# P7 of both layers as an inner Strassen product, and the x1 outer sums on GpSimd, in a two-layer graph kernel

## The chip, the cores and the metric

The kernel runs on one core of a Trainium2 chip. The metric is the device time of one execution in microseconds. The kernel before took 1842.32 us as the median of three runs (1842.28 to 1844.9).

Engine names are those of the profile: PE is TensorE (PEld its weight loads), DVE is VectorE, ACT is ScalarE, POOL is GpSimd, SP is SyncE, which here only issues DMAs.

## What is computed

There are 64 graphs of 256 nodes with 512 features each, all in float32. Two layers follow each other, each with a residual connection and a layer norm:

```python
# layer 0; W is (512, 1024)
deg = jnp.sum(adj, axis=-1, keepdims=True)
agg = jnp.einsum('bij,bjf->bif', adj, x) / jnp.maximum(deg, EPS)
cat = jnp.concatenate([x, agg], axis=2)
x = _layernorm(x + relu(jnp.einsum('bnf,of->bno', cat, W)))
# layer 1; X is the new x
q, k = jnp.split(X @ Wqk, 2, axis=-1)
v = X @ Wv
agg = jnp.einsum('bij,bjd->bid', adj, k * mask[:, :, None])
w = inv_scale * mask * jnp.einsum('bid,bid->bi', q, agg)
x = _layernorm(X + softmax(w, axis=1)[:, :, None] * v)
```

## The kernel before

**Algebra.** In layer 0, W splits into a half that acts on x and a half whose product with x is gathered by adj. In layer 1, Wqk is first folded into one 512 x 512 matrix (`weight_product`), so that q times the gathered k becomes x1 times the gathered product. Each layer therefore has one product of x, or x1, with a 512 x 1024 weight, and one product of adj with a result (`gather`). Each of these is done by the Winograd form of Strassen's scheme: seven products P1 to P7 in place of eight, at the cost of sums of the operands and of the results.

**Outer and inner.** The weight product is split into 2 x 2 blocks; this is the outer step. One of its products has a stationary operand from x of 256 features by 256 rows (128 of each of two graphs) and a weight block of 256 x 512. `outer` (line 619) does it directly, as four matmuls of 128x128 by 128x512, two for each graph. `inner` (line 551) does it by a second step of the same scheme, whose rows are the two graphs, whose contraction halves are the two chunks of 128, and whose columns are the two halves of 512: seven matmuls of 128x128 by 128x256. `INNER` (line 26) lists for each layer the products that are inner ones. P6 and P7 are outer in both layers; `product` (line 614) chooses, and takes `outer` as long as the weight's inner sums don't exist (`sides[p]` is not yet a dict).

**What an inner product needs.** Its weight sums are made once, in `weight_sums` (line 466), by VectorE, or by GpSimd for the products in `W1_BY_GP`. Layer 1's sums of the products in `FULL_FIRST` are kept back in `waiting_sums` and made within the second iteration (line 1025), so that the first pair's layer 1 does these as outer products. Its input sums are made for every pair by GpSimd in `inner_sums` (line 512): four additions of 128x128 for each product, or of 128x256 for P1 and P2 together. In `inner`, each matmul writes half of a scratch bank, and ACT and VectorE carry the result to the target banks `q`. For P4, P6 and P7 (`also`) the target already holds a partial sum:

```python
def third():
    mm(lo, s(2), b["T3"])
    if also:
        vec.tensor_add(halves(q[1]), halves(q[1]), twice(kept(lo)))
```

Here `kept` is an ACT copy of 256 columns into a `fifth` buffer. In all, an inner product with `also` has four such copies, four VectorE additions of 256 columns and one of 512. The sums of the outer step are made in `outer_sums` (line 502), three additions of 512 columns: for x by GpSimd, but for the very first pair, and for x1 by VectorE (line 1008, and in the last pair's part). The fourth one is made in `fourth_sums` by GpSimd.

**Order of the work.** The loop runs over 32 pairs of graphs. An iteration interleaves layer 0 of pair j with layer 1 of pair j-1. The order of PE's units is written out by hand in strings: `ORDER0` and `ORDER1` for the first two iterations, `ORDER` for the others, `ORDER9` for the last pair's layer 1. Each letter is one unit of a product:

- layer 0: i, k, m, p, q, r, s are P1, P5, P2, P6, P7, P3, P4, and a to g are its gather;
- layer 1: J, K, H, Q, N, P, L are P1, P2, P6, P7, P5, P4, P3, and A to G are its gather;
- in the last part, S and Z are two steps of the last softmax.

`take` (line 890) calls the units in this order, and `when` adds work of other engines as soon as named units are done: `start_layer1` after L, P7's input sums of layer 1 after K. Nothing is issued at once. Every instruction goes to the `Plan` (line 75), which gives each a cost and a due time and then writes the order of all engines by list scheduling, PE's included, so that a unit that can't start yet may be passed by a later one. `HOME` and `HOME9` name the scratch bank of each product and each gather, one of eight PSUM banks. [...]

Of the kernel before, what the change touches and what calls it, by code (L numbers as in the profile page):

```python
# [16 lines left out]
P = 128  # L17
Q = 32
# [4 lines left out]
S1, S2, S3, S4 = range(4)  # L23


INNER = (("P1", "P2", "P5", "P3", "P4"), ("P1", "P2", "P5", "P3", "P4"))
SLOTS_X = {"P1": 0, "P2": 1, "P5": 2, "P3": 2, "P6": 0, "P7": 1, "P4": 0}
SLOTS_X1 = {"P1": 0, "P2": 1, "P5": 2, "P6": 0, "P7": 1, **({"P3": 2, "P4": 0} if "P7" in INNER[1] else {"P3": 0, "P4": 1})}
W1_BY_GP = ("P5", "P3", "P4")
HOME = "i6 k7 m6 p2 q0 r7 s6 a7 b2 c3 J6 K2 H4 Q7 N7 L7 P6 A6 B4 C5"  # L30
HOME9 = "J6 K7 H2 Q1 N7 L1 P1 A2 B3 C1"
LATE = 4.0
FULL_FIRST = ("P7", "P4")
ORDER0 = ("k k k k k k i i i i i k i i p p q q r p p r r m m q m m r q m r m r s s s r s m a s b s d s e c "
          "g f")
ORDER1 = ("i k i i i i k k k i k k i p k m m p p r m q p r m r m r q r s r q q s s m r s m s s a J s b d J "
          "J e J J J J c H f H K H K g K Q K K K K C N A Q N N D H N N E N Q B Q P G P N L P L F L P L L L "
          "L")
ORDER = ("i i i k i i k k i i k k k k p p p r q p m m m r m q r m s q r q r s m s s r s s m r a J b J J d "
         "J J J s e c J f H K K H K K g K K N Q K H N Q A D N C E N H Q N G N Q P P F P P P N L L L P P B "  # L40
         "L L L L")
ORDER9 = ("J J A D C E J J J J F J K G B H H K K K H Q K H N Q K Q K P Q N P N P N P P N P P S N N L L L L "
          "Z L L L")


class Step:
# [274 lines left out]
def resnorm_kernel(  # L321
# [13 lines left out]
    B, N, F = x.shape  # L335
    A = wqk_t.shape[0] // 2
    NT, NF, NA = N // P, F // P, A // P
    H, HF = NF // 2, F // 2
# [12 lines left out]
    vec = Recorder(plan, "DVE", nc.vector, vec_cost)  # L351
    act = Recorder(plan, "ACT", nc.scalar, act_cost)
    gp = Recorder(plan, "POOL", nc.gpsimd, gp_cost)
# [110 lines left out]
    waiting_sums = {}  # L464

    def weight_sums(w, name, layer, by_gp=()):
        b11, b21, b12, b22 = (w[:, k * H:(k + 1) * H, :] for k in range(4))
        t1, t2, t4 = (mem.tile([P, H, F], F32, name=f"{name}{k}") for k in (1, 2, 4))
        it = [mem.tile([P, len(INNER[layer]), HF], F32, name=f"{name}i{r}") for r in (1, 2, 4)]
        sides = {"P4": t4, "P6": t2, "P7": b12}  # L470
        sub = vec.tensor_sub

        def inner_of(p, b, later=None):
            later = layer == 1 and p in FULL_FIRST if later is None else later
            if p not in INNER[layer]:
                return
            n = INNER[layer].index(p)
            sub = gp.tensor_sub if p in by_gp else vec.tensor_sub
            c11, c12, c21, c22 = (b[:, e, h * HF:(h + 1) * HF] for e in range(2) for h in range(2))
            i1, i2, i4 = (i[:, n] for i in it)  # L480
            if later:
                waiting_sums[p] = lambda: inner_of(p, b, False)
                return
            sides[p] = {"B11": c11, "B21": c21, "B22": c22, "T3": c12, "T1": i1, "T2": i2, "T4": i4}
            sub(i1, c12, c11)
            sub(i2, c22, i1)
            sub(c12, c22, c12)
            sub(i4, c21, i2)
        sub(t1, b12, b11)
        inner_of("P1", b11)  # L490
        sub(t2, b22, t1)
        inner_of("P5", t1)
        sub(b12, b22, b12)
        sub(t4, b21, t2)
        inner_of("P2", b21)
        inner_of("P6", t2)
        inner_of("P7", b12)
        inner_of("P3", b22)
        inner_of("P4", t4)
        return sides  # L500

    def outer_sums(X, eng):
        eng.tensor_add(X.block(S1), X.block(A21), X.block(A22))
        eng.tensor_sub(X.block(S2), X.block(S1), X.block(A11))
        eng.tensor_sub(X.block(S3), X.block(A11), X.block(A21))
# [421 lines left out]
    for j in range(NP):  # L927
        X = Xs.pop(j)
        own = owns[j] = ring("own", [P, 2, NT, F], 3)
        u, y, o = pf, py, pu  # L930
        ys[j] = ring("y", [P, 2, NT, F])
        at = homes(HOME)
        units, made = layer0(j, X, o, u, y, at), Counter()
        sizes = Counter({name: len(parts) for name, parts in units.items()})
        waiting = []

        def when(done, work):
            waiting.append((full(done, sizes), work))

        def start_gather0():  # L940
            units.update(gather("abcdefg", sumsA.pop(j), sums_T(ys[j]), at["a"], at["c"], at["b"],
                                own=own, rdeg=rdegs.pop(j)))

        def end_gather0():
            place = norm0(j)
            mask_adj(j)
            if place:
                when("P.L" if j else "", place)

        def x_sums(*ps):  # L950
            for p in ps:
                if p in INNER[0]:
                    inner_sums(X, p)

        def next_x():
            if j == 0:
                pass
            elif j < NP - 1:
                load_xT(j + 1)
            if j < NP - 1:  # L960
                inner_sums(Xs[j + 1], None)
                outer_sums(Xs[j + 1], gp)
                inner_sums(Xs[j + 1], "P5")

        def next_adj():
            if j < NP - 1:
                load_adj(j + 1)
                sumsA[j + 1] = adj_sums(j + 1, 0)
        if j > 0:
            load_x(j)  # L970
        if 0 < j < NP - 1:
            load_rows(j + 1)
            degrees(j + 1)
        when("k", lambda: (fourth_sums(X), x_sums("P3")))
        when("i", lambda: x_sums("P6"))
        when("m", lambda: x_sums("P7"))
        when("p" if "P6" in INNER[0] else "i", lambda: x_sums("P4"))
        when("pqr", start_gather0)
        when("rs", next_x)
        when("abcdefg", end_gather0)  # L980
        if j == 0:
            when("abcdefg", next_adj)
        else:
            Y = x1Ts.pop(j - 1)
            u2, o2, y2 = o, pf, y
            vs[j - 1], aggs[j - 1] = v_of(j - 1), agg_of(j - 1)
            q_at = ys[j][:, :, 0]
            new, dots = layer1(j - 1, Y, q_at, o2, u2, y2, at)
            sizes.update({name: len(parts) for name, parts in new.items()})
            made["L"] = sizes["L"] - len(ahead)  # L990
            ahead += new.pop("L")
            units.update(new, L=ahead)

            def y_sums(*ps):
                for p in ps:
                    if p in INNER[1] and isinstance(W1[p], dict):
                        inner_sums(Y, p)

            def start_layer1():
                if j == 1:  # L1000
                    for k in range(2):
                        turn_here(Y, owns[0], k, o)
                    mask_adj(0)
                else:
                    softmax(j - 2)
                sumsM[j - 1] = adj_sums(j - 1, 1)
                inner_sums(Y, None)
                outer_sums(Y, vec)
                inner_sums(Y, "P5")

            def start_gather1():
                units.update(gather("ABCDEFG", sumsM.pop(j - 1), T[0], at["A"], at["C"], at["B"],
                                    aggs[j - 1]))
            when("L" if j > 1 else "m", start_layer1)
            when("J", lambda: y_sums("P6"))
            when("K", lambda: y_sums("P7" if "P7" in INNER[1] else "P4"))
            when("H", lambda: (fourth_sums(Y), y_sums("P4" if "P7" in INNER[1] else "P3")))
            if "P7" in INNER[1]:
                when("HN", lambda: y_sums("P3"))
            T = []  # L1020
            when("ikmpqrs" if j == 1 else "", lambda: T.append(sums_T(owns[j - 1], aggs[j - 1])))
            when("gK", start_gather1)
            when("BFK", dots)
            if j == 1:
                when("QP", lambda: [waiting_sums[p]() for p in sorted(waiting_sums)])
            when("ABCDEFG", next_adj)
        take((ORDER0, ORDER1)[j] if j < 2 else ORDER, units, made, waiting)
        if j > 0:
            py, pu = pu, py
# [34 lines left out]
    def divide():  # L1064
# [12 lines left out]
        ("BFK", dots))]  # L1077
    take(ORDER9, units, Counter(), waiting)
    p = small("probs", [P, 2, NT], 2)
# [51 lines left out]
```

## Time and profile before

| what | value |
|---|---|
| median of the runs | 1842.32 us |
| the profiled execution | 1844.13 us |
| its span, first to last instruction | 1842.4 us |
| granted TensorE clock, mean | 0.997 |
| instructions in the span | 26290 |
| DMA traffic | 181.61 MB, mean 99 GB/s |

The profile is a page on one execution. Its parts used below are: the busy time of each engine with its share of the span; the chain of work that ended last, followed back from the last instruction, as shares by engine; the groups of instructions, each with the tile it writes and those it reads, its shape, its count, its busy time and the mean duration of one in ns, and after the bar the idle time just before them with what ended it; and the waits, as "waiter <- releaser: us in total, times, longest". Since nearly every instruction is issued by one helper, all lines show the same few line numbers, and groups are told apart by their tiles: `bank` is PSUM, `xT` and `x1T` the transposed inputs of the two layers, `_s` their outer sums, `_i` their inner sums, `w` the weights, `t` and `t_i` the weights' sums, `fifth` the copies made by `kept`, `sa` the sums of adj.

### The profile page before, as it was taken

What the parts mean: (1) busy time and instruction counts of PE and PEld (TensorE: products, weight loads), DVE (VectorE), ACT (ScalarE), POOL (GpSimd) and SP (SyncE); (2) the same over time, 40 slices, a digit from 0 to 9 for tenths busy, and PEclk for the clock granted to TensorE, in tenths of its full rate; (3) what the DMA queues carried; (4) which work ended last, traced back from release to release, by engine and by line L of the source; (5) the groups of instructions that cost most, each with busy time, mean ns of one, the idle gap of its engine ahead of it and who ended that gap; (6) DMA issues with size and microseconds to landing.
All of it is one profiled execution on the core that took longest, in us unless ns stands there. A gap on an engine that the chain in (4) does not pass through costs nothing.

```text
span 1842.4 us, 26290 instructions
## 1 busy us (share of the span) xinstructions
PE 1829.1 (99%) x7376; PEld 1381.8 (75%) x7376; DVE 1542.9 (84%) x3397; ACT 1243.4 (67%) x3239; POOL 957.5 (52%) x1519
## 2 busy tenths in 40 slices
PE   9999999999999999999999999999999999999997
PEld 5677777777777777777777777777777777777775
DVE  7888888888889888888888798888888888988877
ACT  3656876667776667766677766677666677666766
POOL 6746454465454564544654545645446545456432
PEclk9999999999999999999999999999999999999998
DMA  6134334334334343343343343433333433434302
GB/s 236 51 76 121 94 93 102 89 108 110 97 81 110 90 118 97 93 98 96 101 114 95 82 107 97 111 99 92 97 99 98 106 104 82 106 97 110 98 13 75
DMA packets 380721, 181.61 MB, mean 99 GB/s; under 512 B 263712, under 2 KB 345248, under 8 KB 380576
## 3 DMA queue, kind: packets, MB, share of 16 engines
q1 hardware_dynamic: 380576, 179.94, 36.6%
q8 instruction: 59, 0.97, 0.2%
q14 instruction: 86, 0.70, 0.1%
HBM read 114.35 MB, written 34.08 MB: 81 GB/s over the span
## 4 chain that ended last, share of the span: by engine, by line
PE 98%; DVE 1%; DMA 1%; ACT 0%; SPq 0%; issue 0%; DVEq 0%; ACTq 0%
PE bank L370 97%; DMA shared<-wqk_t 1%; DVE bank L285 0%; DVE own L285 0%; PE bank L376 0%; SPq L386 0%; ACT own L285 0%; DVE w L285 0%; DVE y L285 0%; DVE x1T_s L285 0%; DVE t L285 0%; ACT fifth L285 0%; DVE x L285 0%; ACT junk L285 0%; ACT bank L285 0%
## 5 line engine op out<-in xcount | busy, mean ns | idle before, releaser
L285 ACT COPY y<-bank 128x512 f32<-128x512 f32 x256 | 146.4, 585 | 369.1 <-PE bank L370 361.5
L285 DVE TENSOR_TENSOR bank<-bank,fifth 128x256 f32<-128x256 f32 x571 | 255.7, 454 | 50.3 <-ACT fifth L285 22.9
L285 POOL TENSOR_TENSOR x1T_i<-x1T 128x256 f32<-128x256 f32 (+1 forms) x126 | 74.8, 605 | 409.4 <-PE bank L370 399.9
L285 ACT COPY shared<-bank 128x512 f32<-128x512 f32 x314 | 183.7, 586 | 74.5 <-PE bank L370 70.3
L370 PE MATMUL bank<-w,x1T 128*128 128x512 f32 (+1 forms) x512 | 207.3, 487 | 1.2 <-DVE own L285 0.7
L370 PE MATMUL bank<-w,xT 128*128 128x256 f32 (+1 forms) x496 | 200.1, 486 | 0.0
L285 ACT ACTIVATE own<-own,shift,rstd 128x512 f32<-128x512 f32 x254 | 197.9, 820 | 1.5 <-DVE shift L285 1.5
L285 ACT ACTIVATE junk<-own,less 128x512 bf16<-128x512 f32 x254 | 183.9, 724 | 4.0
L285 ACT COPY fifth<-bank 128x256 f32<-128x256 f32 x380 | 136.2, 375 | 66.1 <-PE bank L370 62.2
L370 PE MATMUL bank<-t_i,x1T_i 128*128 128x256 f32 x636 | 179.7, 380 | 0.0
L285 ACT COPY bank<-bank 128x256 f32<-128x256 f32 (+1 forms) x352 | 150.5, 428 | 43.0 <-PE bank L370 29.3
L285 DVE SCALAR_TENSOR_TENSOR own<-bank,rdeg,own 128x256 f32<-128x256 f32 x384 | 172.7, 477 | 7.8 <-PE bank L370 2.8
L285 DVE TENSOR_TENSOR shared<-bank,shared 128x512 f32<-128x512 f32 (+1 forms) x157 | 137.7, 892 | 46.4 <-PE bank L370 46.3
L370 PE MATMUL bank<-t_i,xT_i 128*128 128x256 f32 x640 | 165.2, 379 | 0.0
L370 PE MATMUL bank<-t,x1T_s 128*128 128x512 f32 (+1 forms) x384 | 163.6, 521 | 0.6 <-DVE x1T_s L285 0.6
L285 DVE TENSOR_TENSOR y<-bank,y 128x512 f32<-128x512 f32 x192 | 132.0, 688 | 37.1 <-PE bank L370 32.8
L370 PE MATMUL bank<-t,xT_s 128*128 128x512 f32 (+1 forms) x384 | 153.8, 521 | 0.0
L370 PEld LDWEIGHTS bank<-t_i,xT_i 128*128 128x128 f32 x640 | 119.8, 190 | 34.4 <-issue 17.0
L285 POOL TENSOR_TENSOR sa<-adj 128x256 f32<-128x256 f32 x128 | 93.7, 732 | 99.0 <-ACT adj L285 94.5
L285 DVE TENSOR_TENSOR shift<-less,rstd 128x2 f32<-128x2 f32 (+1 forms) x128 | 46.4, 380 | 113.6 <-ACT rstd L285 113.5
L285 POOL TENSOR_TENSOR xT_i<-xT 128x128 f32<-128x128 f32 (+1 forms) x126 | 80.2, 637 | 114.3 <-PE bank L370 103.3
L370 PEld LDWEIGHTS bank<-t_i,x1T_i 128*128 128x128 f32 x636 | 120.1, 190 | 19.7 <-issue 2.2
(170 smaller groups left out, 4589.7 us busy)
## 6 DMA issues: line engine op xcount, KB each, us to landing
x<-x SPq DMA_DIRECT2D x64, 512.0 KB, 3.7
xT<-x_t SPq DMA_DIRECT2D x62, 512.0 KB, 3.8
out<-own SPq DMA_DIRECT2D x62, 512.0 KB, 2.8
x1T<-turn SPq DMA_DIRECT2D x480, 64.0 KB, 2.1
adj<-adj_t SPq DMA_DIRECT2D x64, 256.0 KB, 3.0
turn<-adj SPq DMA_DIRECT2D x64, 256.0 KB, 3.7
turn<-dram SPq DMA_DIRECT2D x31, 264.0 KB, 5.1
shared<-wqk_t SPq DMA_DIRECT2D x4, 512.0 KB, 8.4
```

The costliest lines, as they stand in the source:

```text
L285: self.plan.record(self.name, lambda: call(out, *args, **kwargs), outs, ins, busy, done, port)
L370: plan.record("PE", lambda: nc.tensor.matmul(ps, a, b, start=start, stop=True, skip_group_check=True), [ps], [a, b], busy, busy + 0.165, w ...
```

## The change

P7 becomes an inner product in both layers. This adds its weight sums (layer 1's are made in the second iteration, now after Q, P, N and J in place of Q and P) and its input sums on GpSimd. In layer 1 it also puts P3's and P4's input sums into other slots and makes them one hook later. The x1 outer sums go from VectorE to GpSimd, but for the last pair. The strings that order the units and name the scratch banks are new. The new default in `sides` has no effect on what is issued.

```diff
-INNER = (("P1", "P2", "P5", "P3", "P4"), ("P1", "P2", "P5", "P3", "P4"))
+INNER = (("P1", "P2", "P5", "P3", "P4", "P7"), ("P1", "P2", "P5", "P3", "P4", "P7"))
-HOME = "i6 k7 m6 p2 q0 r7 s6 a7 b2 c3 J6 K2 H4 Q7 N7 L7 P6 A6 B4 C5"
-HOME9 = "J6 K7 H2 Q1 N7 L1 P1 A2 B3 C1"
+HOME = "i6 k7 m7 p0 q6 r7 s6 a7 b2 c3 J3 K2 H5 Q5 N7 L6 P7 A6 B4 C5"
+HOME9 = "J7 K6 H4 Q6 N7 L7 P0 A2 B3 C1"
-ORDER0 = ("k k k k k k i i i i i k i i p p q q r p p r r m m q m m r q m r m r s s s r s m a s b s d s e c "
-          "g f")
-ORDER1 = ("i k i i i i k k k i k k i p k m m p p r m q p r m r m r q r s r q q s s m r s m s s a J s b d J "
-          "J e J J J J c H f H K H K g K Q K K K K C N A Q N N D H N N E N Q B Q P G P N L P L F L P L L L "
-          "L")
-ORDER = ("i i i k i i k k i i k k k k p p p r q p m m m r m q r m s q r q r s m s s r s s m r a J b J J d "
-         "J J J s e c J f H K K H K K g K K N Q K H N Q A D N C E N H Q N G N Q P P F P P P N L L L P P B "
-         "L L L L")
-ORDER9 = ("J J A D C E J J J J F J K G B H H K K K H Q K H N Q K Q K P Q N P N P N P P N P P S N N L L L L "
-          "Z L L L")
+ORDER0 = ("i k k i i i i i k i k k m m m k p m k p m p m m r p q r q q q r r r r q q r q s s s s s a b s s "
+          "d e c f g")
+ORDER1 = ("i k k i i k i k i k i i p m m k k m m p m m p p r r m q q r q r q q r q r q r s s s a J s J s s "
+          "J s b J d J J e c J H f H K K H H K g Q K K K K Q N P C A N B Q D N E Q N G N F N N L L P L P L "
+          "P L L")
+ORDER = ("k k k k i i i L i i i i k m k p k m m p m m q r p p m r r m q q q q q q s s r r s r r s a J s J "
+         "J s s b d J e J g J c f J J K H K H K K H K K K H A N Q Q Q N Q N Q Q N D N C E Q F P P P G P B N "
+         "P N L P L P L L L L")
+ORDER9 = ("J J J J J J J C A D K K E B K K H F G K H Q N H N K H K N N N Q Q Q Q Q N Q P N L P P L L P P P "
+          "L P S L Z L L")
...
-        sides = {"P4": t4, "P6": t2, "P7": b12}
+        sides = {"P1": b11, "P2": b21, "P3": b22, "P4": t4, "P5": t1, "P6": t2, "P7": b12}
...
                 inner_sums(Y, None)
-                outer_sums(Y, vec)
-                inner_sums(Y, "P5")
+                outer_sums(Y, gp)
+                y_sums("P5")
...
-                when("QP", lambda: [waiting_sums[p]() for p in sorted(waiting_sums)])
+                when("QPNJ", lambda: [waiting_sums[p]() for p in sorted(waiting_sums)])
```

More of the change, by code (lines that the diff above doesn't have):

```diff
@@ L29 @@
 W1_BY_GP = ("P5", "P3", "P4")
-HOME = "i6 k7 m6 p2 q0 r7 s6 a7 b2 c3 J6 K2 H4 Q7 N7 L7 P6 A6 B4 C5"
-HOME9 = "J6 K7 H2 Q1 N7 L1 P1 A2 B3 C1"
+HOME = "i6 k7 m7 p0 q6 r7 s6 a7 b2 c3 J3 K2 H5 Q5 N7 L6 P7 A6 B4 C5"
+HOME9 = "J7 K6 H4 Q6 N7 L7 P0 A2 B3 C1"
 LATE = 4.0
 FULL_FIRST = ("P7", "P4")
-ORDER0 = ("k k k k k k i i i i i k i i p p q q r p p r r m m q m m r q m r m r s s s r s m a s b s d s e c "
-          "g f")
-ORDER1 = ("i k i i i i k k k i k k i p k m m p p r m q p r m r m r q r s r q q s s m r s m s s a J s b d J "
-          "J e J J J J c H f H K H K g K Q K K K K C N A Q N N D H N N E N Q B Q P G P N L P L F L P L L L "
-          "L")
-ORDER = ("i i i k i i k k i i k k k k p p p r q p m m m r m q r m s q r q r s m s s r s s m r a J b J J d "
-         "J J J s e c J f H K K H K K g K K N Q K H N Q A D N C E N H Q N G N Q P P F P P P N L L L P P B "
-         "L L L L")
-ORDER9 = ("J J A D C E J J J J F J K G B H H K K K H Q K H N Q K Q K P Q N P N P N P P N P P S N N L L L L "
-          "Z L L L")
+ORDER0 = ("i k k i i i i i k i k k m m m k p m k p m p m m r p q r q q q r r r r q q r q s s s s s a b s s "
[4 more added lines that the diff above has]
+ORDER = ("k k k k i i i L i i i i k m k p k m m p m m q r p p m r r m q q q q q q s s r r s r r s a J s J "
+         "J s s b d e J g J c f J J K H K H K K H K K K H A N Q Q Q N Q N Q Q N D N C E Q F P P P G P B N "
+         "P N L P L P L L L L")
+ORDER9 = ("J J J J J J J C A D K K E B K K H F G K H Q N H N K H K N N N Q Q Q Q Q N Q P N L P P L L P P P "
+          "L P S L Z L L")
 class Step:
```

## The prediction, on record before the result

> **What bounds the kernel now.** I read the page's busy line and its chain of waits first, then busy time by stretch, the order of time on PE, and the groups and waits of the engines that PE depends on.
>
> ```profile
> PE 1829.1 (99%) x7376; PEld 1381.8 (75%) x7376; DVE 1542.9 (84%) x3397; ACT 1243.4 (67%) x3239; POOL 957.5 (52%) x1519
> ...
> PE 98%; DVE 1%; DMA 1%; ACT 0%; SPq 0%; issue 0%; DVEq 0%; ACTq 0%
> ```
>
> PE is busy all the time and carries 98% of the chain that ended last. A busy PE need not be a fast PE, so I looked at where it has gaps:
>
> ```profile
> core 0: us, PE busy (x) PEld busy (x) DVE busy (x) ACT busy (x) POOL busy (x), PEclk, DMA share, GB/s
> 0.00:100.00 100.00, 96.20 (x352) 63.87 (x353) 78.69 (x151) 50.61 (x129) 68.92 (x98) 1.00 0.41 138
> 500.00:1000.00 500.00, 500.00 (x2028) 380.83 (x2027) 423.10 (x940) 342.05 (x899) 261.83 (x420) 1.00 0.38 99
> 1777.00:1842.40 65.40, 55.90 (x227) 40.16 (x226) 44.26 (x110) 45.06 (x117) 17.40 (x30) 0.90 0.16 53
> ```
>
> Only the first 100 us and the last 65 have PE gaps. DVE stands at 423 of 500 us in the steady part. And at what pitch PE runs there:
>
> ```profile
> 600.53 1.03 PE L370 MATMUL bank<-shared,sa 128*128 128x256 f32 x4
> 601.40 0.59 PE L370 MATMUL bank<-t_i,x1T 128*128 128x256 f32 x2
> 601.83 0.59 PE L370 MATMUL bank<-t_i,x1T_i 128*128 128x256 f32 x2
> 602.26 1.02 PE L370 MATMUL bank<-w,x1T 128*128 128x512 f32 x2
> 603.12 1.03 PE L370 MATMUL bank<-shared,adj 128*128 128x256 f32 x4
> ```
>
> Each float32 matmul of the code is two records. The starts differ by 0.43 us for a 256-column matmul (601.40 to 601.83) and 0.86 for a 512-column one (602.26 to 603.12). The medians from record to record over the whole trace are 216 and 429 ns. One pair of graphs in the loop has 32 records of 512 columns (P6 and P7 of both layers) and 196 of 256 (five inner products a layer of 7 matmuls, two gathers of 14): 32 x 0.429 + 196 x 0.216 = 56.06 us, and the 1000 us from 500 on, with 4058 records, lose about 3 us against that pitch. The steady part has no slack: less PE work is less time, as long as the others keep up.
>
> ```profile
> L285 DVE TENSOR_TENSOR bank<-bank,fifth 128x256 f32<-128x256 f32 x508 | 212.3, 425 | 50.1 <-ACT fifth L285 22.7 <-PE bank L370 16.6 <-ACT junk L285 1.7
> L285 DVE TENSOR_TENSOR bank<-bank,fifth 128x512 f32<-128x512 f32 x63 | 43.4, 689 | 0.2 <-ACT fifth L285 0.2
> L285 DVE TENSOR_TENSOR x1T_s<-x1T 128x512 f32<-128x512 f32 x32 | 22.2, 693 | 0.1
> L285 POOL TENSOR_TENSOR xT<-xT 128x512 f32<-128x512 f32 x30 | 38.5, 1284 | 0.0
> L285 POOL TENSOR_TENSOR x1T_i<-x1T_s 128x128 f32<-128x128 f32 x128 | 59.6, 467 | 29.2 <-DVE x1T_s L285 26.8
> ```
>
> These are the prices of what the change adds and moves. Last, what DVE waits for from 500 to 1500 us, and one wait of PE's weight load:
>
> ```profile
> DVE shift L285 <- ACT rstd L285: 65.2, 34, 3.6
> DVE shared L285 <- PE bank L370: 27.0, 17, 1.6
> DVE y L285 <- PE bank L370: 18.3, 37, 0.6
> DVE bank L285 <- ACT fifth L285: 11.4, 18, 0.6
> ...
> PEld bank L370 <- POOL xT_i L285: 11.0, 17, 0.7
> ```
>
> [...] of 355 such DVE additions of 512 columns, the 214 that overlap no GpSimd instruction took 682 ns on average, the 141 that do 933. [...]
>
> **The change, part by part.**
>
> *PE.* P7 as an outer product is 8 records of 512 (3.43 us); as an inner one, 14 of 256 (3.02): 0.41 us less. It applies to 32 pairs in layer 0 and to 31 in layer 1, since the first pair's layer 1 is built before the weight sums of P7 exist. 63 x 0.412 = **26.0 us** off PE. A pair goes from 56.06 to 55.24 us.
>
> *DVE.* Inner P7 accumulates on banks that already hold P6, so each of its scratch results is copied by ACT and added by DVE: four additions of 256 and one of 512, 4 x 0.425 + 0.689 = 2.39 us, 4.78 a pair. The x1 outer sums leave: 3 x 0.697 = 2.09. Net +2.69. Contention now costs DVE some 91 us in all (the excess of overlapped over free durations, the 512 ns excess of the tiny shift products included), 2.9 a pair; with GpSimd busier by a quarter and fewer DVE targets I add 0.3. DVE work a pair is 0.848 x 56.06 = 47.5, so 50.5 of 55.24 us: 91%. It lies beside PE's work; that is the cover, and its loss is the first rival below.
>
> *ACT.* Four copies of 375 ns a P7: +3.0 us a pair, 38.4 to 41.4 of 55.2 (75%). They are queued with norm's squares and its rstd, for which DVE's shift waits. I charge nothing: ACT still idles a quarter of the time; uncovered it is up to 3 us a pair.
>
> *GpSimd.* The three outer sums come to 3 x 1.284 = 3.85 us, the sums of P7's inputs to 8 x about 0.5 = 4.0: 29.2 to 37.1 a pair, 67%. What is queued behind the outer sums is P5's sums (4 x 0.467) and later those of P4, P7, P3; in exchange GpSimd's own wait for DVE's S1 (26.8 us in the row above) goes. Covered, since in the new order J comes 39 units of at least 0.43 us, 17 us, after the L that starts them; uncovered, P5 would be 1.8 us later (3.85 against 2.09).
>
> *Scratch banks.* P7 of both layers now needs one (q6, Q5), shared with i6 and s6, and with the gather's C5. A P7's units can't run tighter than matmul, copy, next matmul; the trace has no such inner P7. Bounds: 0 if other products lie between, as they do for P4 now, to about 0.3 us for each of three reuses (copy 0.375 plus the matmul's tail, less one unit of 0.43), 0.9 a product, 1.8 a pair. For this and all other small waits of the steady part I take 0.15 us a pair near the lower end, because units of N, r or p can be put between: 30 x 0.15 = **+4.5 us**.
>
> *Head.* Layer 0's P7 weight sums are four more DVE subtractions of 256 (the t_i and w rows of the first 35 us take 0.41 to 0.67): 2.1 us, plus 2.39 for the first q, in 100 us with 78.7 of DVE work and 3.8 of PE gaps. Between 0 and 4.5; I take **+1.5**. Layer 1's sums come at about 140 us behind other DVE work, first read by the next pair: nothing.
>
> *Tail.* The last pair has 2.39 us more on DVE, where DVE and ACT set the end from 1818 us on (0 to +3). Against this its new order leaves 3 L units after S in place of 9 N and L units, and those 9 ran from 1825 to 1834.5 with gaps: S comes some 2 us later, what follows ends some 4 earlier (-2). I take 0.
>
> *Orders.* Otherwise the same units in new places: no charge beyond the 0.15 above, as the old order left PE without gaps and the new one must be as good; uncovered, that is the rivals. DMA volume and SP's queue don't change.
>
> *Sum.* The profiled execution took 1844.13 us (span 1842.4, 1.7 around it): 1844.1 - 26.0 + 4.5 + 1.5 + 0 = 1824.1. It lies 1.8 above the median of the runs shown, 1842.32, so in terms of the median **1822.3**.
>
> **Rivals.**
>
> *DVE becomes the bound (slower).* DVE idles about 7.5 us a pair at waits, 3.65 of them with shift at the head of its queue until ACT has rstd (65.2 us over 17.8 pairs). DVE work 50.5 + 0.3 of small gaps + waits: if the waits stay over 5.3 us a pair, the pair is longer than 56.06 and the gain is gone. At 6 us: 56.8, +0.75 x 30 = +22, and with the head +1.5, near 1866. For it: shift's wait isn't one for PE, and ACT gets 3 us more ahead of it; DVE is at 94 to 100% in more than half of the stretches of 4 us of a pair. Against it: waits for PE shrink by themselves when DVE is behind, and most norm and transpose work of DVE isn't urgent.
>
> *GpSimd comes late (gain half lost).* PE's weight load already waits 0.65 us once a pair for a sum by GpSimd, just hidden. With 7.9 us more on that queue, 0.4 us more of it uncovered costs 30 x 0.4 = 12: about 1834. For it: GpSimd is at 90 to 100% in some stretches of a pair. Against it: its longest wait, for PE, is 13 us once a pair.
>
> *P7 isn't replaced.* Only so for the first pair's layer 1, counted above.
>
> **Chances and range.** Forecast, 1814 to 1830: 0.50. GpSimd or bank waits, 1830 to 1846: 0.20, of which 0.12 still faster. DVE-bound, slower: 0.30, half of it over 1862. A measurement of this kernel tells about 0.2%, 3.7 us, from no change. So faster 0.62, same 0.08, slower 0.30. The low end takes no stalls and the better tail (1844.1 - 26.0 - 2 - 1.8 = 1814); the high end goes into the slower case to leave out less than 0.2.
>
> **What would show it.** Right: 256-column records up by 882, 512 down by 504; PE without gaps from 100 us to the tail, a pair near 55.3 us; DVE at 91% and GpSimd at 67% there, DVE's waits for PE smaller. Wrong: PE gaps every pair released by DVE bank (first rival) or by POOL x1T_i or xT_i (second), or by ACT fifth (scratch bank), each read as PE idle over 30 pairs; head and tail by the first 100 and last 65 us.

## The result and the profile after

The changed kernel takes 1842.75 us (median of 12 runs, 1842.14 to 1843.51); beside it the kernel before takes 1842.7 us (12 runs, 1841.92 to 1844.9). The ratio is 0.9999, 95% interval 0.999 to 1.0008: no change, where a gain of 20 us was forecast. The profiled execution took 1842.84 us, its span is 1841.0 us.

Busy line and chain shares of the page, after:

```profile
PE 1818.4 (99%) x7754; PEld 1433.2 (78%) x7754; DVE 1672.4 (91%) x3627; ACT 1332.0 (72%) x3491; POOL 1269.4 (69%) x1864
...
PE 96%; DVE 2%; ACT 1%; DMA 0%; issue 0%; POOL 0%; SPq 0%; ACTq 0%; DVEq 0%
```

378 records of 882 - 504 more: the replacement of P7 happened in full. DVE is at 91% and GpSimd at 69%, as forecast. PE is still busy 99% and still carries the chain. Yet 26 us of its work are gone and the time stayed, so PE got slower somewhere. Busy time by stretch (columns as in the prediction) shows only part of where:

```profile
0.00:100.00 100.00, 94.31 (x358) 64.34 (x359) 80.99 (x158) 49.90 (x127) 73.08 (x102) 1.00 0.39 133
500.00:1000.00 500.00, 500.00 (x2147) 397.75 (x2146) 462.22 (x1003) 370.62 (x974) 353.53 (x521) 1.00 0.38 101
1777.00:1841.00 64.00, 49.00 (x225) 39.34 (x223) 46.74 (x115) 45.38 (x121) 18.07 (x31) 0.91 0.17 54
```

The first 100 us have 5.7 us of PE gaps in place of 3.8, the last stretch 15.0 of 64.0 in place of 9.5 of 65.4. In the steady part PE is busy 500.00 of 500 us, in both kernels. **The count in brackets tells more than the busy time.** A pair has 228 records before and 240 after; at their pitch alone (56.06 and 55.24 us a pair) 500 us would hold 228 x 500 / 56.06 = 2034 and 240 x 500 / 55.24 = 2172. Before has 2028 of them, after 2147. So before loses 0.3% and after 1.2%, in gaps too short to show as idle time.

To place the loss I took one mark in every pair but the last, DVE's transpose of the softmax (`turned<-wide`, 31 marks), and cut the span at the second and at the fourth mark from the end:

| us | before | after | difference |
|---|---|---|---|
| start to second mark (head) | 173.59 | 178.87 | +5.3 |
| 26 pairs between (mean of one) | 1461.9 (56.23) | 1453.7 (55.91) | -8.2 |
| fourth mark from the end to the end (tail) | 206.87 | 208.41 | +1.5 |
| span | 1842.4 | 1841.0 | -1.4 |

Before's profiled execution is 1.4 us longer than the median of its runs, and in its tail the granted clock is 0.50 from 1829.6 us on while PE still works until 1835.4 (in after PE is done when the clock falls), so the table understates what the tail lost.

Of the 63 P7, 52 lie in the 26 pairs (52 x 0.412 = 21.4 us), the others in head and tail. The forecast sum, cut at the same marks, is about 0 for the head, -21.4 + 26 x 0.15 = -17.5 for the middle and -2.3 for the tail. The result falls short of it by 5.3, 9.3 and 3.8 us: three losses, and the experiments take them one by one. In what follows "a pair" is the mean distance of the marks in the middle, from the fifth mark to the fourth from the end: 56.23 us before, 55.90 after.

DVE's longest wait between 500 and 1500 us, and the two waits of PE's weight load that changed most:

```profile
DVE bank L285 <- ACT fifth L285: 15.1, 52, 0.4
```

```profile
PEld bank L370 <- DVE bank L285: 26.0, 73, 0.6
PEld bank L370 <- POOL xT_i L285: 0.2, 1, 0.2
```

The wait of shift for rstd, on which my first rival rested (65.2 us), is gone, the copy into `fifth` is now the longest, and all of DVE's waits together are 61 us, 3.4 a pair. The weight load's wait for GpSimd, the second rival's evidence, went from 11.0 to 0.2 us. New is that weight loads wait for a DVE result four times a pair (0.2 us in all before).

What became dearer is DVE's and GpSimd's work with inputs in SBUF (groups by shape):

```profile
L285 DVE SCALAR_TENSOR_TENSOR own<-own,x 128x512 f32<-128x512 f32 x128 | 131.8, 1033 | 0.0
L285 DVE TENSOR_TENSOR bank<-bank,fifth 128x256 f32<-128x256 f32 x760 | 313.3, 430 | 46.5 <-ACT fifth L285 18.6 <-ACT bank L285 7.0 <-PE bank L370 6.7
L285 POOL TENSOR_TENSOR xT_s<-xT 128x512 f32<-128x512 f32 x30 | 51.0, 1699 | 0.0
```

The first took 911 ns before, the third 1279. The second has one input in PSUM and took 425 before: no change to speak of. The work of DVE a pair went from 47.67 to 51.68 us, 4.0 more where I had +3.0.

One such case in the timeline of after, with what it does to PE (start, duration, engine, operation):

```profile
712.51 1.72 POOL L285 TENSOR_TENSOR xT_s<-xT 128x512 f32<-128x512 f32 x1
713.43 1.35 DVE L285 SCALAR_TENSOR_TENSOR own<-own,x 128x512 f32<-128x512 f32 x1
714.72 0.42 DVE L285 TENSOR_TENSOR bank<-bank,fifth 128x256 f32<-128x256 f32 x1
714.76 0.59 PE L370 MATMUL bank<-w,x1T 128*128 128x256 f32 x2
715.28 0.67 PE L370 MATMUL bank<-t,x1T_i 128*128 128x256 f32 x2
715.78 0.35 ACT L285 COPY fifth<-bank 128x256 f32<-128x256 f32 x1
715.79 0.59 PE L370 MATMUL bank<-shared,sa 128*128 128x256 f32 x2
716.28 1.10 PE L370 MATMUL bank<-t_i,x1T_i 128*128 128x256 f32 x4
```

The first DVE operation takes 1.35 us beside GpSimd's sum instead of 0.68, the mean of the three of them in this trace that overlap no GpSimd instruction. The addition behind it, of the same shape as P7's but of another product (it keeps its 0.42 us in experiment 2), starts at 714.72, though the copy it needs was there at 714.48. PE's matmul that needs a DVE result then starts 0.52 us after the one before it and the next 0.51, in place of 0.43 each: 0.17 us lost, and PE is "busy" throughout. The matmul at 716.28 waits in the same way for ACT's copy of 715.78.

### The profile page after: what moved, and what is told of

It is laid out like the page before. It is cut to its first block, busy times and chain, and to the rows that moved or that the text cites. A ratio compares the mean times of both kernels' runs of the same rounds, so it can differ in the third digit from the quotient of the medians.

```text
span 1841.0 us, 28183 instructions
## 1 busy us (share of the span) xinstructions
PE 1818.4 (99%) x7754; PEld 1433.2 (78%) x7754; DVE 1672.4 (91%) x3627; ACT 1332.0 (72%) x3491; POOL 1269.4 (69%) x1864
## 4 chain that ended last, share of the span: by engine, by line
PE 96%; DVE 2%; ACT 1%; DMA 0%; issue 0%; POOL 0%; SPq 0%; ACTq 0%; DVEq 0%
PE bank L370 96%; DVE own L285 1%; DMA shared<-wqk_t 0%; DVE bank L285 0%; ACT own L285 0%; SPq L386 0%; PE bank L376 0%; DVE tv L285 0%; DVE shared L285 0%; DVE y L285 0%; POOL xT_s L285 0%; DVE w L285 0%; DVE turn L285 0%; DVE x L285 0%; ACT adj L285 0%
## 5 line engine op out<-in xcount | busy, mean ns | idle before, releaser
L285 DVE TENSOR_TENSOR bank<-bank,fifth 128x256 f32<-128x256 f32 x886 | 394.6, 467 | 56.8 <-ACT fifth L285 28.9
L285 ACT COPY fifth<-bank 128x256 f32<-128x256 f32 x632 | 226.9, 376 | 249.0 <-PE bank L370 248.5
L370 PE MATMUL bank<-t_i,x1T_i 128*128 128x256 f32 x760 | 213.2, 382 | 0.4 <-DVE bank L285 0.3
L285 POOL TENSOR_TENSOR x1T_i<-x1T 128x256 f32<-128x256 f32 (+1 forms) x188 | 102.5, 552 | 154.9 <-PE bank L370 151.4
L370 PE MATMUL bank<-t_i,xT_i 128*128 128x256 f32 x768 | 205.6, 383 | 1.3 <-POOL xT_i L285 0.9
L370 PE MATMUL bank<-w,x1T_i 128*128 128x256 f32 x508 | 148.9, 384 | 3.1 <-DVE bank L285 1.7
L285 ACT COPY own<-bank 128x512 f32<-128x512 f32 x192 | 112.5, 587 | 47.7 <-PE bank L370 46.8
L370 PE MATMUL bank<-w,xT_i 128*128 128x256 f32 x512 | 143.0, 383 | 0.6 <-DVE bank L285 0.6
L285 POOL TENSOR_TENSOR xT_i<-xT 128x128 f32<-128x128 f32 (+1 forms) x188 | 103.0, 548 | 54.3 <-PE bank L370 42.7
L285 DVE SCALAR_TENSOR_TENSOR own<-own,x 128x512 f32<-128x512 f32 x128 | 131.8, 1033 | 0.0
```

Of the source, the lines that this page charges most:

```text
L285: self.plan.record(self.name, lambda: call(out, *args, **kwargs), outs, ins, busy, done, port)
L370: plan.record("PE", lambda: nc.tensor.matmul(ps, a, b, start=start, stop=True, skip_group_check=True), [ps], [a, b], busy, busy + 0.165, w ...
```

## The experiments

Each is compared with runs of the kernel before on the same chip (medians 1842.96 to 1843.23 us). "Order kept" means that the planner was given the uncut costs, so that all engines have the same order as in after and only the cut operations are shorter. "..." stands for lines of an edit that are not shown.

**1. x1's outer sums short.** GpSimd's three additions act on a quarter of their columns, from the third pair's iteration on.

```diff
-                outer_sums(Y, gp)
+                outer_sums(Y, gp, 32 if j > 1 else None)
...
```

> The changed kernel with its instruction order kept, but from the second use on GpSimd's three x1 outer sums work on 128 columns in place of 512 (layer 1 is then computed from old sums). It takes some 2.5 us a pair off GpSimd (3.85 to about 1.4) and nothing directly off DVE. Theory (DVE is late, partly through contention with GpSimd): DVE's two-input instructions get shorter, DVE's busy share falls by 1 to 2 points, and the pair goes from 55.90 us to about 55.65: some -7 us in all, near 1835. Rival (GpSimd itself is late, PE waits for its sums): the pair goes to 55.4 and the time to about 1828. Rival (scratch banks): no change, 1842.

Measured 1841.88 us, ratio 0.9994 (0.9985 to 1.0002). A pair takes 55.89 us. GpSimd does 2.8 us a pair less, DVE, freed of some contention, 1.4 less, and PE gains nothing. Both the theory (55.65 us a pair) and the rival of a late GpSimd (55.4) fell. So neither these three sums on GpSimd's queue nor 1.4 us of the amount on DVE sets the time. (P7's input sums, the other part of GpSimd's added work, are not cut here.)

**2. P7's DVE additions short.** They act on 32 or 64 columns, the rest is left out.

```diff
-                vec.tensor_add(q[0][:, :HF], q[0][:, :HF], kept(lo))
+                onto_bank(q[0][:, :HF], kept(lo)[:], few)
...
```

`onto_bank` leaves the additions of other products whole.

> The changed kernel with its order kept, but VectorE's additions of inner P7 (four of 256 columns, one of 512, in both layers) work on 32 or 64 columns, so that P7's results are incomplete. It takes some 1.5 us a P7 off DVE, 3 a pair, and neither GpSimd nor ACT work. Theory (DVE is late): PE's waits for DVE's bank additions go, the pair falls from 55.90 us to the 55.4 that the planner's own schedule has, some -15 us, near 1828; head and tail give back 1 to 3 us more. Rival (GpSimd late): under 3 us of gain, 1840. Rival (scratch banks bound by the copies of ACT): under 5 us, 1838.

Measured 1837.56 us, 0.9972 (0.996 to 0.9984); a pair 55.73 us, 0.17 less, with 3.1 us less DVE work. That is a third of the gain that my theory gave this cut (a pair of 55.4 us).

**3. P7's ACT copies short.** They act on 32 columns.

```diff
-            act.copy(tmp, half)
+            if p == "P7" and rings["fifth", (P, HF)].n > 8:
+                short("ACT", nc.scalar, act_cost, "copy", [tmp[:], half], [tmp[:, :32], half[:, :32]])
+            else:
+                act.copy(tmp, half)
...
```

> The changed kernel with its order kept, but ACT's copies of P7's scratch results work on 32 columns in place of 256 (P7's results are then wrong). It takes about 0.2 us off each of eight copies a pair, and off the time for which a scratch bank is held and DVE waits for the copy. Theory (DVE's amount of work): little, 0 to 4 us of gain, 1839 to 1842. Rival (scratch banks: PE waits for the copy before the next matmul of a P7): 10 us or more, below 1833.

Measured 1839.27 us, 0.9977 (0.9969 to 0.9985); a pair 55.76 us, 0.14 less. I had charged these copies nothing. The gain is of the size that the theory gave, but it comes where the rival put it, at a scratch bank. The copies stand ahead of DVE's additions, yet this 0.14 and the 0.17 of experiment 2 are different time, as the table under experiment 7 shows.

**4. x1's outer sums back on DVE**, planned anew with after's strings.

```diff
-                outer_sums(Y, gp)
+                outer_sums(Y, vec)
```

> The changed kernel with x1's outer sums back on VectorE in all pairs; the planner lists the order anew from the same strings. 2.09 us a pair more on DVE, 3.85 less on GpSimd. Theory (DVE is late): slower, the planner's own schedule has PE gaps of 1.1 to 1.3 us a pair in place of 0.2, so at least +30 us, 1870 to 1890. Rival (GpSimd late or its contention is what costs): faster than the changed kernel, 1830 to 1840.

Measured 1900.11 us, 1.0309 (1.0292 to 1.0327), 57.96 us a pair, slower still than the 1870 to 1890 us expected. This doesn't price the move: the planner wrote another order of all engines with it. It does show how little these strings can be carried over to another division of work.

**5. All of GpSimd's sums short**, 32 columns each from the fourth pair on, order kept.

```diff
+            if self.name == "POOL" and self.plan.few:
+                cut = [few_of(ap_of(a)) for a in (out, *args)]
+                self.plan.record(self.name, lambda: call(*cut, **kwargs), outs, ins, busy, done, port)
+                return
...
+        plan.few = j > 2
```

> The changed kernel with its instruction order kept, but from the fourth iteration on every GpSimd sum (of x, x1 and adj) works on 32 columns of its last dimension, so that results are computed from partly old sums. GpSimd falls from 39.4 us a pair to about 22, and overlaps DVE's two-input instructions much less; DVE's own instructions are the same. With the shorter x1 sums alone the pair stayed at 55.90 us, but the waits of PE that the trace shows begin behind DVE instructions stretched by the sums of x. Theory (contention with GpSimd makes DVE late at single points): DVE falls from 51.7 to about 49.5 us a pair, the pair from 55.90 to 55.6 us or less, near 1833. Rival (the copy-and-add chain of the inner products is longer than the order leaves room for, whatever GpSimd does): the pair stays above 55.8, 1840 or more.

Measured 1833.68 us, 0.9948 (0.9931 to 0.9964). The steady stretch of this kernel:

```profile
500.00:1000.00 500.00, 500.00 (x2160) 401.82 (x2159) 426.78 (x1009) 372.96 (x982) 158.25 (x522) 1.00 0.37 101
```

2160 records where after has 2147; a pair takes 55.59 us, 0.31 less. DVE's own instructions are the same and in the same order, but take 35 us less of the 500; `own<-own,x` falls from 1033 to 731 ns. Time and pair are those that the theory gave, and this is the largest single part of the steady loss. The cut makes GpSimd's own sums come earlier too, but in after PE waits for hardly any of them (the weight load 0.2 us in 1000).

**6. The same cut in the kernel before**, as a control.

> The kernel before, with every sum of GpSimd cut to its first 32 columns from the fourth pair on (so that the sums are wrong beyond these), its order kept: the same cut that took 9.1 us from after. If the contention between GpSimd and VectorE costs TensorE time only since the change, because after's order leaves no margin, this gains little: TensorE loses 0.17 us a pair in before, and at most 0.05 of it is this, so 1841 us, range 1840 to 1843, with a mean distance of pairs of 56.15 to 56.23 us. If the contention cost before as much, it gains some 8 us: 1834.5 us.

Measured 1839.92 us, 0.9981 (0.9975 to 0.9988).

```profile
500.00:1000.00 500.00, 500.00 (x2030) 381.20 (x2029) 400.79 (x940) 342.99 (x901) 119.60 (x422) 1.00 0.38 99
```

Only 2 records more than before's 2028, and 56.14 us a pair, 0.09 less. The time is 0.1 us below the range expected. 2.1 of the 3.6 us that the profiled execution gained lie in the tail (204.8 us in place of 206.9), where its clock is full until 1834.8 us, after PE's last record. In the steady part the contention cost PE 0.09 us a pair before the change and 0.31 after it.

**7. Cuts 2 and 5 together.**

> After, with both cuts at once: GpSimd's sums on 32 columns from the fourth pair on and VectorE's additions of P7 on 32 or 64 columns, the order kept. If what is left of the loss with GpSimd's sums short (55.60 us a pair) is the order's own gaps (planned at 0.20 us a pair) and what was lost in before too (0.17), the second cut adds almost nothing: 55.55 us a pair, 1832.5 us, range 1831 to 1834. If VectorE's amount of work holds TensorE up by itself, the two add up: 0.31 and 0.17 us a pair, some 55.43 us a pair and 1828.5 us.

Measured 1828.57 us, 0.9918 (0.9901 to 0.9934).

```profile
500.00:1000.00 500.00, 500.00 (x2167) 405.17 (x2166) 404.66 (x1013) 374.38 (x983) 158.03 (x522) 1.00 0.38 101
```

A pair takes 55.43 us: the two cuts add up in full (0.31 + 0.17 = 0.48, measured 0.47). My expectation that the second would add almost nothing fell. With both, PE loses 55.43 - 55.24 = 0.19 us a pair, about the 0.17 of the kernel before. The weight load's wait for DVE stays at 25.4 us in this kernel, so that row marks where PE hangs on DVE, and isn't itself the loss.

**Where in the pair the time goes** can be worked out from the starts of PE's records: what lies between two starts beyond 216 ns (after a record of 256 columns) or 429 ns (after one of 512) is lost. Means of 18 pairs in the middle, in ns a pair, of the places that lose over 50 in after. The first column is rounded, 2, 3, 5 and 7 are experiments, "-" is under 8, and the last column is what the records there waited for last, by the semaphores:

| us after the mark, reads | after | 2 | 3 | 5 | 7 | waits for |
|---|---|---|---|---|---|---|
| 10, `w,xT_i` | 59 | - | 58 | 58 | - | DVE, `bank<-bank,fifth` |
| 33, `t,x1T_i` | 166 | 164 | 164 | - | - | DVE, `bank<-bank,fifth` |
| 34, `t_i,x1T_i` | 127 | 128 | - | - | - | ACT, `fifth<-bank` |
| 37, `w,x1T_i` | 97 | - | 97 | 95 | - | DVE, `bank<-bank,fifth` |
| 49, `w,xT` | 56 | 52 | 52 | 56 | 56 | DVE, `bank<-bank,shared` |
| 52, `t_i,xT_i` | 135 | 143 | 143 | 143 | 143 | ACT, `bank<-bank` |

The places at 33 and 34 are those of the timeline above (715.28 and 716.28). Contention costs these two, 0.29 us; P7's additions cost those at 10 and 37, 0.16. At 34 PE waits for one of P7's copies, so experiment 3 recovers a part of what experiment 5 does and nothing of what experiment 2 does. The last two places stay in every cut and are the 0.19 us that is left. None of the six waits for GpSimd. In experiment 1 all six are as in after: what runs beside DVE's 1.35 us is `xT_s<-xT`, a sum of x that GpSimd made before the change too. In before it met `own<-own,x` once a pair as well, which then took 1668 ns (mean of 27), and all of the contention cost PE 0.09 us there (experiment 6). So it is not the meeting alone that sets the loss, but how soon behind it a reader on PE stands in the order.

**8. Tail: the last pair's P7 by one step**, with the old order of the last part. In this build P3's scratch bank is one that the last softmax writes as well, so the last pair's output is changed.

```diff
-        if p in INNER[layer] and isinstance(sides[p], dict):
+        if p in INNER[layer] and isinstance(sides[p], dict) and not (p == "P7" and outer_p7):
...
```

> The changed kernel, but with the last pair's layer 1 as before the change: P7 outer (its weight block is restored by one VectorE subtraction), and the old order of the last part. 0.41 us more on PE. Theory (the last pair's chain P1, P6, P7, P4 to the softmax runs on one pair of banks, and an inner P7 lengthens it by its copies and additions): the stretch from the last pair's softmax of the pair before to the end falls from 42.6 us to about 40, the time to 1840. Rival (the 2.8 us that the tail lost have another cause, such as DVE's amount of work carried over from the loop): the stretch stays at 42 to 43 us, 1842 to 1843.

Measured 1840.57 us, 0.9987 (0.998 to 0.9994). The stretch that the theory names falls from 42.6 to 40.6 us, as forecast. From the fourth mark before the end to the end it is 206.94 us, 1.5 less than after. This and the next experiment take back P7 and the last part's order together, so they don't tell one from the other.

**9. The same with a scratch bank of its own** (`HOME9` with L1 and P1).

> The last pair's P7 of x1's layer alone goes by one step, with scratch banks that nothing else of the tail writes; all else is that of after. If the tail's loss is the serial chain P1, P6, P7, P4, softmax on one pair of banks, the run from the last softmax transpose but one to the end gets back 2 to 3 us: 1840.3 us, range 1839 to 1841.5, and the time from the last record of TensorE to the end falls from 12.3 to about 7 us. If the end is set by the work that follows the softmax instead, nothing changes: 1842.7 us.

Measured 1841.96 us (1840.06 to 1845.0, 20 runs), 0.9994 (0.9987 to 1.0). The profiled execution took 1840.06 us, 2.8 less than after's, of which 1.7 in the tail, with 8.2 us from PE's last record to the end in place of 12.3; the median of the runs is only 0.8 below after's, over the range expected (the last section has what sets these runs apart). So the direction is as expected and the size unsettled. What the tail hangs on can be read in after's trace all the same, PE and ACT in the last 20 us:

```profile
1821.50 0.70 PE L370 MATMUL bank<-t_i,x1T 128*128 128x256 f32 x2 [1.01 <-DVE bank L285]
1823.92 0.60 PE L827 MATMUL bank<-ident,w 128*1 128x128 f32 x4 [0.30 <-DVE w L285]
1827.69 0.70 PE L370 MATMUL bank<-t_i,x1T_s 128*128 128x256 f32 x2
1828.32 0.60 PE L370 MATMUL bank<-total,fifth 1*128 1x1 f32 x4
```

```profile
1825.07 0.20 ACT L285 ACTIVATE less<-sum 128x2 f32<-128x2 f32 x1 [4.97 <-DVE own L285]
```

and in that of before:

```profile
1825.05 0.60 PE L827 MATMUL bank<-ident,w 128*1 128x128 f32 x4 [0.21 <-DVE w L285]
1834.22 1.22 PE L370 MATMUL bank<-t_i,x1T_s 128*128 128x256 f32 x2 [0.79 <-DVE bank L285]
```

The `ident,w` matmul is the step S. PE's last group of records came 5.9 us earlier than before (1834.22 to 1828.32), but S only 1.1 (1825.05 to 1823.92), since PE waits for DVE four times on the way to it and to the last sums. From S to the end it takes 17.1 us, before 17.3: ACT, idle for 4.97 us until 1825.07, then has the norms to do one after another. Part of before's 17.3 us is the half clock: its last two matmul records take 1.22 us, after's of the same kind 0.70. In experiment 6, with before's order and a full clock while PE works, S to the end takes 15.6 us. At equal clock, then, the last part became longer by 1.5 us, and not just no shorter.

**10. P7 inner in the middle only**: experiment 8, and in the first two iterations P7 of layer 0 outer too, with head orders near those of before. Two scratch banks in the first iterations are accumulators of other products in this build, so the first pairs' output is changed.

```diff
-        when("m", lambda: x_sums("P7"))
+        when("m", lambda: x_sums("P7") if j > 1 else None)
...
-        at = homes(HOME)
+        at = homes(HOME_HEAD if j < 2 else HOME)
```

> P7 inner only where the loop is in its steady state: the last pair's layer 1 as in the run before, and in the first two iterations layer 0's P7 outer too, with its weight sums put off to the second iteration and with strings for these two iterations near the old ones. The steady order is the changed kernel's. PE does 0.82 us more than in the run with the last pair alone. Theory (the changed kernel's head is late because layer 0's P7 sums and additions come before DVE has anything to spare, and because the units of an inner P7 can't be hidden while the pipeline fills): the second softmax comes at about 174 us in place of 178.9, the pair stays at 55.9, the tail at 40.6, and the time is 1835 to 1837, faster than both kernels. Rival (the head's loss comes from the x1 sums on GpSimd, or from the loop's order reaching into the head): the second softmax stays near 178, 1840.

Measured 1835.73 us (5 runs), 0.9959 (0.9945 to 0.9972); second mark at 173.03 us, 5.8 earlier than after.

**11. The same as a whole kernel**, with experiment 9's tail, other banks in the head and a few units of `ORDER1` exchanged for them.

```diff
...
+HOME_HEAD = "i6 k7 m6 p2 q0 r7 s6 a7 b2 c3 J6 K2 H4 Q7 N7 L7 P6 A6 B4 C5"
-HOME9 = "J7 K6 H4 Q6 N7 L7 P0 A2 B3 C1"
+HOME9 = "J7 K6 H4 Q6 N7 L1 P1 A2 B3 C1"
...
```

> P7 stays by the second step in both layers from the third pair on; in the first two pairs P7 of x's layer, and in the last pair P7 of x1's layer, go by one step again, with orders and scratch banks of their own for those pairs; what is computed is the reference's. The steady order is that of after. If the gain was lost in the head (5.3 us), in the tail (2.8 us) and in the steady part (some 15 us), this one gets back the first two: 1842.7 - 5.3 - 2.8 + the P7 records of three halves of a pair taken back (about 3 x 5 x 0.412 / 2 = 0.6 to 1.2 us each way) = 1835.5 us, range 1833.5 to 1838, the second transpose of the softmax at some 173 us, the mean distance of pairs between unchanged at 55.9 us. If instead the steady part alone holds the loss and the head and the tail are only moved about, it stays at 1840 to 1843 us.

Measured 1837.69 us (1835.78 to 1839.58, 6 runs), 0.9969 (0.9958 to 0.9981): 5.4 us faster than the kernel before, and 5.1 than after. Nothing of the computation is left out or changed in it. The second mark is at 172.81 us, 6.1 earlier than after, a pair at 55.91; the tail, 208.2 us, gave back nothing this time (its clock falls to 0.50 at 1820.8 us, and PE works until 1827.6). Its head against after's (two stretches, after first):

```profile
14.00:65.00 51.00, 48.68 (x188) 34.56 (x189) 44.91 (x90) 32.66 (x91) 41.70 (x60) 1.00 0.53 177
65.00:157.50 92.50, 89.50 (x370) 66.49 (x368) 79.67 (x166) 54.72 (x140) 68.58 (x90) 1.00 0.21 55
```

```profile
14.00:65.00 51.00, 49.45 (x189) 34.44 (x188) 43.22 (x85) 31.50 (x88) 40.17 (x57) 1.00 0.51 173
65.00:157.50 92.50, 92.36 (x385) 70.83 (x384) 81.46 (x173) 59.37 (x154) 68.49 (x95) 1.00 0.22 61
```

After has PE gaps of 5.3 us in these 143.5, the whole kernel of 11 only 1.7, the kernel before 2.2. Of what ends after's gaps there, the three largest:

```profile
PE bank L370 <- DVE w L285: 1.4, 1, 1.4
PE bank L370 <- DVE own L285: 1.0, 2, 0.7
PE bank L370 <- POOL xT_i L285: 0.9, 1, 0.9
```

`w` is a sum of layer 1's weights for P2, which before has too, but at 87.3 us, and after at 92.5, behind DVE work that now comes ahead of it; `xT_i` are input sums. In the kernel of 11 and in before no matmul of this stretch waits for either. That leaves some 2.4 us of the head's 6.1 which no gap shows. Experiments 10 and 11 take back P7 and the head's orders together, so which of the two costs more stays open; the x1 sums on GpSimd, which both keep, are not it.

## Why the prediction was wrong

**PE, -26.0 us: right.** All the records went, and in experiment 7, where the other engines have less to do, a pair comes down to 55.43 us.

**DVE, +2.69 and 0.3 for contention: the first term right, the second mis-sized.** The counts are as given (252 more additions of 256, 63 more of 512, x1's sums moved). Contention grew by some 1.5 us a pair, not 0.3: DVE's excess over free durations went from 91 to some 138 us. Additions of 512 columns with two inputs in SBUF took 682 ns free and 951 overlapped, about as before, but 230 of 262 were overlapped, against 141 of 355. I had scaled contention by GpSimd's busy time; by these counts it went with how many DVE instructions met it. GpSimd's three added sums were mis-sized a little too: 4.2 us (1272, 1299 and 1581 ns) in place of 3.85.

**The cover of this work failed**, though DVE at 91% was as forecast. It wasn't the first rival either: no pair is longer than before, DVE idles still, and 1.4 us less of its work brought nothing (experiment 1). What counts is the single result that PE waits for. The step that failed is "**for this and all other small waits of the steady part I take 0.15 us a pair**": it is 0.49 (0.82 - 0.33). By the runs this is 0.31 - 0.09 = 0.22 for contention with GpSimd over what it cost before, 0.17 for P7's additions on DVE, and 0.10 that is left, at two places that wait for a DVE result and an ACT copy whatever was cut. Behind it stands "the old order left PE without gaps and the new one must be as good". By the costs in the kernel's own planner, which are no measurement, the number of PE units a pair that start within 0.3 us of the first moment that the DVE result they need allows rose from 6 to 18, and the planned end fell only from 1837.7 to 1825.8 us. The order itself promised 12 us, not 26, and that could have been read before.

**ACT, nothing, and the scratch banks near 0: wrong by a little.** A copy of P7's costs 0.13 us a pair, at a place where PE waits for the scratch bank. In after ACT makes that copy just after a wait of 0.35 us for DVE's `own`; with GpSimd's sums short PE's wait is gone as well.

**GpSimd late: didn't come.** In the steady part PE waits for hardly any of its sums (0.2 us in 1000); the price was paid by DVE instead.

**Head, +1.5: mis-sized.** 5.3 at the mark, 6.1 against experiment 11. I counted DVE's added work but not that sums which were there before come later behind it, and that PE waits for them; how much of this is P7 and how much the new order is open.

**Tail, 0: wrong by 3.8.** "S comes some 2 us later" held: measured from the fourth mark from the end, 191.3 against 189.6 us. "What follows ends some 4 earlier" failed. Fewer L units after S shorten PE's part, and PE isn't the end of this chain; the norms on DVE and ACT are.

Sum: -20.0 forecast; 9.3 in the middle, 5.3 in the head and 3.8 in the tail were missed; -1.4 came. Between the medians it is 0.0: the difference is the half clock in the tail of before's profiled execution, so the tail's loss against a run of before at full clock is larger than 3.8. That three losses just use up the gain is chance: taking the head's away (experiment 11) leaves 5.4 us.

Open are what in the new order makes the two places wait that no cut removed, which part of the head's loss is P7's and which the order's, and the tail's size. Among GpSimd's sums it is one of x, `xT_s<-xT`, that the trace shows beside DVE's late instructions; no experiment cut it alone. A steady order with more room between DVE's results and PE wasn't tried.

## What to carry to other kernels

When an engine at 99% gets less to do, ask of each result it waits for how much room is left, not how busy the others are on average: here short delays at single results took 60% of the gain of a pair (0.49 of 0.82 us). Count records per stretch against their pitch, since busy time hides such losses (500.00 of 500 us on PE in both kernels here, with 0.3% and 1.2% lost). Cost the start and the end as stages of their own, and use the faster form only where its extra preparation and its longer chain are covered.

## What had not been expected of the hardware

**Contention works both ways and reaches far.** Both engines can pay: DVE's `own<-own,x` takes 731 ns with GpSimd's sums short and 1033 in after, GpSimd's `xT_s<-xT` 1279 in before and 1699 in after. Where the two overlap, `own` takes 1668 ns and `xT_s` 1279 in before, `own` 1162 (mean of 57) and `xT_s` 1708 (mean of 29) in after. In experiment 1, with GpSimd's x1 sums short, DVE won back 1.4 us a pair from 2.8 us of GpSimd's.

**The end of the kernel is partly run at half the TensorE clock, from a point that varies.** The granted clock falls from 1.00 to 0.50 at 1829.6 us in before, at 1829.4 in after and at 1820.8 in experiment 11. PE is at work ahead of the fall: it is busy for 2.99 of the last 4 us before it in before, for 3.07 in after, and for 1.20 of the 2 us from 1818 on in experiment 11. What sets the point is not shown. In experiment 11, as in before, the clock is 0.50 while PE still has sums to make, in after only behind its last one (experiment 11 first):

```profile
1824.00:1826.00 2.00, 1.54 (x4) 0.67 (x2) 1.26 (x5) 1.95 (x7) 0.00 (x0) 0.50 0.28 104
```

```profile
1830.00:1832.00 2.00, 0.00 (x0) 0.00 (x0) 2.00 (x7) 1.52 (x7) 0.00 (x0) 0.50 0.00 0
```

Of the 20 runs of experiment 9, the 8 with a mean clock of 0.998 or more took 1840.1 to 1841.2 us, the 12 others 1841.8 to 1845.0. Of the 23 runs of before beside experiment 6, the 14 at 0.998 or more took 1841.9 to 1843.3 us, the 9 others 1844.1 to 1845.1. Differences of 1 or 2 us in the tail are therefore hard to tell.
